# Turning the rounded values by VectorE blocks and DMAs over DRAM instead of the DMA transpose, with the linear layer four places later

## The chip, the core and the metric

The kernel runs on one core of a Trainium2 chip. The core has five engines that run side by side and wait for one another through semaphores: TensorE (PE: matmuls; its weight loads are shown as PEld), VectorE (DVE), ScalarE (ACT), GpSimd (POOL) and SyncE (SP), which issues all the DMAs of this kernel from one queue. The metric is the device time in microseconds (us) of one execution; a comparison takes the median of several runs of each kernel.

## The reference

Sixteen sequences of 256 rows and 256 channels pass through one block: normalise, attention with a mask that leaves 4 sink positions and a window of 32, a projection, and then a linear layer that works on values rounded to 8 bits.

```python
def attention(x, wq, wk, wv, wo):              # x: (16, 256, 256), already normalised
    q = heads(x @ wq.T, 16); k = heads(x @ wk.T, 4); v = heads(x @ wv.T, 4)   # heads of 128
    scores = q @ k.T / sqrt(128)
    mask = (k_pos <= q_pos) & ((k_pos < 4) | (k_pos >= q_pos - 31))
    return merge(masked_softmax(scores, mask) @ v) @ wo.T

def linear(x, weight, bias):                   # x already normalised
    w_scale = max(abs(weight), axis=1) / 127;  w_q = clip(round(weight / w_scale), -128, 127)
    x_scale = maximum(max(abs(x), axis=2) / 127, 1e-12);  x_q = clip(round(x / x_scale), -128, 127)
    return (x_q @ w_q.T) * x_scale * w_scale + bias

x = x + attention(layernorm(x), wq, wk, wv, wo)
x = x + linear(layernorm(x), weight, bias)
```

## The kernel before

The work is cut into 128 units: 16 sequences (n), 4 groups of heads (g), 2 tiles of 128 rows (t). The main loop at the end of the kernel (line 915) walks over them; its index i is called a place here, and a sequence takes 8 places (`PER`). What belongs to other sequences is hung into the places by `at(slot, f, what)`: `small` steps run at the end of a place, `begin` steps early in it, after the read of the weights that the place before wrote, and `close` steps only in the last place. Behind place 124 the `small` steps run in the middle of the place, before the weights are normalised. Every engine runs its instructions in the order in which they were written down (`in_written_order`).

In a place, PE computes the scores of its unit (`pss`, line 560), parts of the output projection of earlier units (`py`), the attention outputs of the unit two places back (`po`, line 623), in every second place a chunk of keys or values (`pk`, `pv`) of the coming sequence, and two heads of its queries (`pq`). Most products are done with seven block products in place of eight, whose sums VectorE and POOL put together (lines 306 to 310). VectorE takes the scores out (571), finds their maximum (573), ScalarE takes the exponentials (598), VectorE divides (605 to 617) and turns the weights in blocks of 32x32 (582). The turned weights travel through DRAM: `zd<-z` (584) at the end of the place, `ad<-zd` (588) early in the next; `po` uses `ad` another place later. The units from 123 on are turned by PE instead (`ptd`, line 565, interleaved with the scores) and used in the very next place.

The normalised input of a coming sequence (`xn`) is turned the same way by `turned_by_blocks`: a block transpose on VectorE (389), four DMAs out to DRAM (394), and, one place later, four DMAs back (403). The first two sequences are turned on PE.

The linear layer of a finished sequence n is `ffn_steps(n)`: statistics, norm (193), scale (714), rounding (721 on VectorE, clamp and subtraction on POOL, 724 and 725, the latter into a bf16 tile `h16`), a transposing DMA from `h16` into `hT` (728), four bf16 matmuls against the rounded weights (`pa`, 739), two evictions on VectorE (`y`, 744), an addition on POOL (745) and the store (746). These six steps stand 4, 5, 6, 8, 9 and 10 places after the end of the sequence. For n = 14 they stand in the places 124 to 127, with the transpose among the `begin` steps of 127 and the matmuls among its `close` steps. The last sequence, 15, has a path of its own (`last_steps`).

Of the kernel before, what the change touches and what calls it, by code (L numbers as in the profile page):

```python
# [9 lines left out]
FP = mybir.dt.float32  # L10
BF = mybir.dt.bfloat16
# [23 lines left out]
def kernel(  # L35
# [12 lines left out]
    pe, dve, act, pool, sp = nc.tensor, nc.vector, nc.scalar, nc.gpsimd, nc.sync  # L48
    B, T, DM = x.shape
    P = 128  # L50
# [4 lines left out]
    NC = DM // P  # L55
    NT = T // P
# [4 lines left out]
    QB = 32  # L61
# [9 lines left out]
    SCALE = 1.0 / math.sqrt(D)  # L71

    const = ctx.enter_context(tc.tile_pool(name="const", bufs=1))
    xp = ctx.enter_context(tc.tile_pool(name="xp", bufs=5))
    p1 = ctx.enter_context(tc.tile_pool(name="p1", bufs=1))
    p2 = ctx.enter_context(tc.tile_pool(name="p2", bufs=2))
    p3 = ctx.enter_context(tc.tile_pool(name="p3", bufs=3))
    dram = ctx.enter_context(tc.tile_pool(name="dram", bufs=3, space=bass.MemoryType.DRAM))
# [4 lines left out]
    ps_m = ctx.enter_context(tc.tile_pool(name="ps_m", bufs=2, space=bass.MemoryType.PSUM))  # L83
# [40 lines left out]
    ident16 = const.tile([P, P], BF, name="ident16")  # L124
# [53 lines left out]
    def statistics(src, tiles, tag, eng=pool):  # L178

        st = p2.tile([P, NT, nc.vector.BN_STATS_DIM], FP, tag="st", name=f"st_{tag}")  # L180
        mv = p3.tile([P, NT, nc.vector.BN_AGGR_DIM], FP, tag="mv", name=f"mv_{tag}")
        for j in tiles:
            dve.bn_stats(st[:, j, :], src[:, j, :])
        for j in tiles:
            dve.bn_aggr(mv[:, j, :], st[:, j, :])
        js = slice(tiles[0], tiles[-1] + 1)
        eng.tensor_scalar(mv[:, js, 1], mv[:, js, 1], LN_EPS, None, ALU.add)
        pool.tensor_tensor(mv[:, js, 1], mv[:, js, 1], half[:, js], ALU.pow)
        return mv

    def standardise(dst, src, mv, tiles):
        for j in tiles:
            dve.tensor_scalar(dst[:, j, :], src[:, j, :], mv[:, j, 0:1], mv[:, j, 1:2], ALU.subtract, ALU.mult)


    wqfT = const.tile([P, NC, DM], BF, name="wqfT")
# [139 lines left out]
    xns, xnT, qt, kt, vw, xn_sums, mvs = {}, {}, {}, {}, {}, {}, {}  # L336
# [22 lines left out]
    def norm_steps(n):  # L359
        def stats():  # L360
            mvs[n] = statistics(xts[n], range(NT), f"a{n}")

        def norm(t):
            if t == 0:
                xns[n] = p1.tile([P, NT, DM], FP, tag="xn", name=f"xn_{n}")
            standardise(xns[n], xts[n], mvs[n], [t])

        return [stats, lambda: norm(0), lambda: norm(1)]

    def channels(n):  # L370

        xn_sums[n] = p2.tile([P, 4, P], FP, tag="xs4", name=f"xs4_{n}")
        b = xn_blocks(n)
        right_sums([xn_sums[n][:, i] for i in range(4)], *b[0], *b[1])

    def turned(n):
        xnT[n] = p2.tile([P, NC, T], FP, tag="xnT", name=f"xnT_{n}")
        pt = ps_m.tile([P, NC, T], FP, tag="m", name=f"xt_{n}")
        for c in range(NC):
            for j in range(NT):  # L380
                pe.transpose(pt[:, c, j * P : (j + 1) * P], xns[n][:, j, c * P : (c + 1) * P], ident)
        dve.tensor_copy(xnT[n], pt)
        channels(n)

    def turned_by_blocks(n):


        z = p1.tile([P, NQ, NT * NC, QB], FP, tag="zx", name=f"zx_{n}")
        dve.transpose(z, xns[n].rearrange("p t (c q i) -> p q (t c) i", c=NC, q=NQ))
        zd = dram.tile([P, NQ, NT * NC, QB], FP, tag="zx", name=f"zxd_{n}")  # L390

        def out():
            for a in range(NQ):
                sp.dma_start(
                    zd[:, a].rearrange("(q j) k i -> j q (k i)", q=NQ),
                    z[a * QB : (a + 1) * QB].rearrange("j q k i -> j q (k i)"),
                )

        def back():
            xnT[n] = p2.tile([P, NC, T], FP, tag="xnT", name=f"xnT_{n}")  # L400
            for t in range(NT):
                for c in range(NC):
                    sp.dma_start(
                        xnT[n][:, c, t * P : (t + 1) * P].rearrange("p (a i) -> p a i", a=NQ), zd[:, :, t * NC + c]
                    )

        return out, back

    NQ = P // QB
# [285 lines left out]
    def ffn_steps(n):  # L695
        xt = xts[n]
        tiles, tag = range(NT), f"{n}"
        h = p1.tile([P, NT, DM], FP, tag="h", name=f"h_{tag}")
        h16 = p1.tile([P, NT, DM], BF, tag="h16", name=f"h16_{tag}")
        xs = p2.tile([P, NT], FP, tag="xs", name=f"xs_{tag}")  # L700
        hT = p1.tile([P, NT, NC, P], BF, tag="hT", name=f"hT_{tag}")
        y = p1.tile([P, NT, DM], FP, tag="yo", name=f"y_{tag}")
        got = []

        def stats():
            got.append(statistics(xt, tiles, f"f{tag}"))

        def norm():
            standardise(h, xt, got[0], tiles)
            if n < B - 2:  # L710
                add_bias(pool)

        def scale():
            dve.tensor_reduce(xs, h, AX.X, ALU.max, apply_absolute_value=True)
            dve.tensor_scalar(xs, xs, 1.0 / 127.0, 1e-12, ALU.mult, ALU.max)

        def quantise():
            xr = p2.tile([P, NT], FP, tag="xr", name=f"xr_{tag}")
            dve.reciprocal(xr, xs)
            for j in tiles:  # L720
                dve.scalar_tensor_tensor(
                    h[:, j, :], h[:, j, :], xr[:, j : j + 1], magic.to_broadcast([P, DM]), ALU.mult, ALU.add
                )
            pool.tensor_scalar(h, h, MAGIC + 127.0, MAGIC - 128.0, ALU.min, ALU.max)
            pool.tensor_scalar(h16, h, MAGIC, None, ALU.subtract)

        def turn():
            sp.dma_start_transpose(
                hT.rearrange("p j c t -> p (j c) t"), h16.rearrange("p j d -> p (j d)")
            )  # L730

        def add_bias(eng):
            eng.tensor_add(xt, xt, bias_bc.unsqueeze(1).to_broadcast([P, NT, DM]))

        def linear():
            pa = ps_m.tile([P, NT, DM], FP, tag="m", name=f"pa_{tag}")
            for j in tiles:
                for c in range(NC):
                    pe.matmul(  # L739
                        pa[:, j, :], hT[:, j, c], wqfT[:, c, :],  # L740
                        start=(c == 0), stop=(c == NC - 1),
                    )
            for j in tiles:
                dve.scalar_tensor_tensor(y[:, j, :], pa[:, j, :], xs[:, j : j + 1], wsc_bc, ALU.mult, ALU.mult)
            pool.tensor_add(y, y, xt)
            sp.dma_start(out_v[n], y)

        return [stats, norm, scale, quantise, turn, linear, lambda: add_bias(dve)]

    def last_steps(j):  # L750

# [72 lines left out]
    begin, close, chunks, early, asked, shares, small, later = {}, {}, {}, {}, {}, {}, {}, {}  # L824

    def at(slot, f, what=small):
        what.setdefault(slot, []).append(f)

    for n in range(B):
        q = (-3, -2, -1, 0, 1, 2, 3, 4)  # L830
        if n == 0:
            q = (-1, -1, 0, 0, 1, 1, 2, 4)
# [10 lines left out]
    for n in range(1, B):  # L843
        first = n * PER - 14
        places = (0, 1, 1, 2) if n == 1 else (4, 5, 6, 7) if n == 2 else (first - 2, first + 2, first + 4, first + 5)
        for k, slot in enumerate(places[:3]):
            at(slot, lambda n=n, k=k: norm_steps(n)[k]())
        if n == 1:
            at(places[3], lambda n=n: turned(n))
        else:  # L850
            def turn(n=n, slot=places[3]):
                for k, f in enumerate(turned_by_blocks(n)):
                    at(slot + 1 + k, f, begin)
                at(slot + 2, lambda: channels(n))

            at(places[3], turn)
            at(max(first - 4, 0), lambda n=n: load_x(n))
# [19 lines left out]
    for n in range(B - 1):  # L877
        done = (n + 1) * PER

        slots = (4, 5, 6, 8, 9, 10) if n < B - 2 else (4, 5, 6, 6, 7, 7, 7)  # L880
        for k, slot in enumerate(slots):
            def step(n=n, k=k):
                if k == 0:
                    steps[n] = ffn_steps(n)
                steps[n][k]()
            at(done + slot, step, begin if k == 4 and n == B - 2 else close if k == 5 and n == B - 2 else small)


    warm = ps_m.tile([P, P], FP, tag="m", name="warm")
# [25 lines left out]
    for i in range(len(units) + 2):  # L915
# [43 lines left out]
        for n, h in asked.pop(i, []):  # L959
            f = queries(n, h)  # L960
# [57 lines left out]
```

## Time and profile before

| | us |
|---|---|
| median of three runs | 769.09 (767.9 to 769.29) |
| the profiled execution | 767.44 |
| its span, first to last instruction | 765.7 |
| PE, share of the chain that ended last | 96% |
| one sequence in the middle | 46.1 |
| in it: PE, VectorE, POOL, ScalarE busy | 46.1, 39.3, 32.2, 24.5 |
| DMA engines busy in the middle | 45% |

A profile line of the timeline gives start, duration, engine, source line, operation, what is written from what, the number of merged instructions, and in brackets the idle time before it and what ended it. A line of the groups gives the shapes, the count, the busy time, the mean duration in ns, and the idle time ahead of the group. A line of the waits gives the total, the number and the longest. A line that lists one tile's instructions gives the shortest, median and longest duration in ns and the first and last start. SP's lines are the issuing of a DMA, not its landing.

### The profile page before, as it was taken

To read this page: it belongs to the slowest core of one execution; us is meant where nothing else is said; L and a number is where in the kernel's file an instruction comes from. 1 tells how busy PE (TensorE), PEld (TensorE's weight loads), DVE (VectorE), ACT (ScalarE), POOL (GpSimd) and SP (SyncE) were. 2 spreads that over 40 slices of the span, in tenths; PEclk is the share of its full clock that TensorE was granted. 3 is DMA by queue.
4 is the path that set the end of the run, shared out by engine and by line. 5 is a ranking of instruction groups with operands and counts; after the bars stand their busy time and mean duration, and the time that the engine had idled before them with its cause. 6 is when DMAs were issued, how large, how long until landed. Compare 5 with 4: busy or idle time off the path is not lost.

```text
span 765.7 us, 18824 instructions
## 1 busy us (share of the span) xinstructions
PE 754.4 (99%) x6483; PEld 742.4 (97%) x6483; DVE 621.8 (81%) x1775; ACT 399.2 (52%) x1561; POOL 511.7 (67%) x812
## 2 busy tenths in 40 slices
PE   9999999999999999999999999999999999999995
PEld 7999999999999999999999999999999999999994
DVE  2588888888888888888888888888888888778765
ACT  3555555555455454555555455554545555455551
POOL 4666977676675867757676675866758676675622
PEclk9999999999999999999999999999999999999998
DMA  7634354344544425445344543436344354443310
GB/s 241 215 102 129 106 147 140 107 124 118 154 124 133 131 90 163 128 137 144 100 125 128 147 141 123 129 96 163 120 145 135 99 136 128 130 137 105 100 40 31
DMA packets 150679, 97.45 MB, mean 127 GB/s; under 512 B 44984, under 2 KB 148792, under 8 KB 150584
## 3 DMA queue, kind: packets, MB, share of 16 engines
q1 hardware_dynamic: 150584, 96.24, 42.8%
q8 instruction: 52, 0.85, 0.5%
q14 instruction: 43, 0.35, 0.2%
HBM read 54.39 MB, written 39.85 MB: 123 GB/s over the span
## 4 chain that ended last, share of the span: by engine, by line
PE 96%; DVE 2%; DMA 1%; ACT 0%; POOL 0%; issue 0%; DVEq 0%; POOLq 0%; ACTq 0%
PE pq L527 24%; PE py L678 23%; PE po L623 15%; PE pss L560 14%; PE pk L495 6%; PE pv L507 6%; PE py L662 3%; PE pq L538 2%; PE pa L739 1%; DMA ad<-zd 1%; PE warm L891 1%; PE pv L470 0%; PE pk L461 0%; PE ptd L565 0%; ACT scores L598 0%
## 5 line engine op out<-in xcount | busy, mean ns | idle before, releaser
L598 ACT ACTIVATE scores<-scores,nmax 128x68 f32<-128x68 f32 x512 | 173.5, 340 | 247.2 <-DVE nmax L573 244.8
L623 PE MATMUL po<-ad,vw 96*128 96x128 f32 x1024 | 135.4, 275 | 0.4 <-DMA ad<-zd 0.4
L560 PE MATMUL pss<-kt,qt 128*128 128x68 f32 x1024 | 130.2, 268 | 0.0
L623 PEld LDWEIGHTS po<-ad,vw 96*128 96x128 f32 x1024 | 125.6, 192 | 1.5 <-DMA ad<-zd 0.5
L560 PEld LDWEIGHTS pss<-kt,qt 128*128 128x128 f32 x1024 | 126.1, 192 | 0.7 <-issue 0.5
L527 PE MATMUL pq<-xs,wq_sums 128*128 128x128 f32 x714 | 118.6, 275 | 0.0
L571 DVE SCALAR_TENSOR_TENSOR scores<-pss,masks 128x272 f32<-128x272 f32 x128 | 56.2, 439 | 63.7 <-PE pss L560 60.8
L527 PEld LDWEIGHTS pq<-xs,wq_sums 128*128 128x128 f32 x714 | 98.8, 192 | 0.0
L598 ACT ACTIVATION_READ_ACCUMULATOR scores<-scores,nmax 128x1 f32 x512 | 95.6, 187 | 0.0
L635 ACT COPY oT<-po 128x512 f32<-128x512 f32 x129 | 75.4, 585 | 23.0 <-PE po L623 23.0
L678 PE MATMUL py<-wo_sums,os 128*128 128x128 f32 x672 | 87.0, 279 | 0.0
L257 POOL TENSOR_TENSOR os<-oT 128x256 f32<-128x256 f32 x56 | 41.0, 732 | 58.0 <-ACT oT L635 58.0
L678 PEld LDWEIGHTS py<-wo_sums,os 128*128 128x128 f32 x672 | 79.5, 192 | 0.0
L306 POOL TENSOR_TENSOR ktmp<-b_k 128x256 f32<-128x256 f32 x30 | 22.4, 746 | 84.3 <-ACT b_k L327 84.3
L527 PE MATMUL pq<-xnT,wq_sb 128*128 128x128 f32 x476 | 72.7, 275 | 0.1
L582 DVE STREAM_TRANSPOSE z<-scores 128x384 f32<-128x384 f32 x120 | 69.4, 578 | 4.1
L617 DVE TENSOR_TENSOR scores<-scores,sm 128x272 f32<-128x272 f32 x120 | 60.3, 503 | 4.1
L527 PEld LDWEIGHTS pq<-xnT,wq_sb 128*128 128x128 f32 x476 | 62.7, 192 | 0.2 <-PE pv L507 0.2
L678 PE MATMUL py<-wo_sb,oT 128*128 128x128 f32 x448 | 62.0, 281 | 0.0
L573 DVE TENSOR_REDUCE nmax<-scores 128x4 f32<-128x272 f32 x128 | 55.8, 436 | 4.4
L678 PEld LDWEIGHTS py<-wo_sb,oT 128*128 128x128 f32 x448 | 54.5, 192 | 0.0
L308 DVE TENSOR_TENSOR qt<-pq,qt 128x256 f32<-128x256 f32 x119 | 50.5, 424 | 4.0
(187 smaller groups left out, 1700.4 us busy)
## 6 DMA issues: line engine op xcount, KB each, us to landing
zd<-z SPq DMA_DIRECT2D x120, 192.0 KB
ad<-zd SPq DMA_DIRECT2D x120, 192.0 KB
vd<-vt SPq DMA_DIRECT2D x30, 256.0 KB
vw<-vd SPq DMA_DIRECT2D x30, 256.0 KB
vw<-vd SPq DMA_DIRECT2D x30, 224.0 KB
x<-in_x_dram SPq DMA_DIRECT2D x15, 256.0 KB
out_dram<-y SPq DMA_DIRECT2D x15, 256.0 KB
zxd<-zx SPq DMA_DIRECT2D x56, 64.0 KB
```

The source lines that it names most:

```text
L308: eng.tensor_add(c21_c22, like(p[1][:, 0:2], c21_c22), v.unsqueeze(1).to_broadcast(c21_c22.shape))
L495: pe.matmul(to, left, right, start=True, stop=True)
L527: pe.matmul(to, left, right, start=True, stop=True)
L560: pe.matmul(pss[:, k, :], qt[n, g][:, t, k].rearrange("p h i -> p (h i)"), kt[n, g][:, t * NBLK + k, :], start=True, stop=True,)
L571: dve.scalar_tensor_tensor(s[:, :, 0:NK], pss, SCALE, masks[:, t], ALU.mult, ALU.add)
L573: dve.tensor_reduce(nmax, s[:, :, 0:NK], AX.X, ALU.max, negate=True)
L582: dve.transpose(z, s.rearrange("p k (c i) -> p c k i", c=NCH))
L598: act.activation(s[:, k, 0:NK], s[:, k, 0:NK], AF.Exp, bias=nmax[:, k : k + 1], scale=1.0, accum_out=sm[:, k : k + 1],)
L617: dve.tensor_mul(s, s, sm.unsqueeze(2).to_broadcast([P, NBLK, NK]))
L623: pe.matmul(po[:, k], vw[n, g // 2][:, t * NBLK + k, g % 2 * D : (g % 2 + 1) * D], ad[:, :, k], start=True, stop=True,)
L635: act.copy(o[:, t, hs].rearrange("p h (k i) -> p k h i", i=QB), po[:, :, hs])
L678: pe.matmul(region(py, i), left[:, e], right[:, e], start=(g == 0 and e == 0 and i in (1, 4)), stop=(g == G - 1 and e == 1 and i in (7, 3)),)
```

## The change

The rounded values of the sequences 0 to 13 are no longer narrowed to bf16 by POOL and transposed by a DMA. POOL leaves them in f32 in place. VectorE turns them in blocks of 32x32 (the same helper as for the normalised input, now with the source, the pool and a tag as arguments), four DMAs carry them out to DRAM and four back, and ScalarE narrows the result to bf16 (`narrow`). That takes nine steps instead of six; they stand 4, 5, 6, 8, 10, 11, 12, 13 and 14 places after the end of the sequence, so that the matmuls stand at 14 in place of 10. For n = 13 the turn and all after it stand one place earlier, and the matmuls at place 125 (112 + 13). Sequence 14 keeps the bf16 tile and is turned by four PE transposes at the beginning of place 127, narrowed by ScalarE out of PSUM. The pool of inputs `x` gets a sixth buffer, since an input is held longer. The layout of `hT` changes from row tile first to channel half first.

```diff
-    xp = ctx.enter_context(tc.tile_pool(name="xp", bufs=5))
+    xp = ctx.enter_context(tc.tile_pool(name="xp", bufs=6))
...
-    def turned_by_blocks(n):
+    def turned_by_blocks(src, pool_of, tag):
-        z = p1.tile([P, NQ, NT * NC, QB], FP, tag="zx", name=f"zx_{n}")
-        dve.transpose(z, xns[n].rearrange("p t (c q i) -> p q (t c) i", c=NC, q=NQ))
-        zd = dram.tile([P, NQ, NT * NC, QB], FP, tag="zx", name=f"zxd_{n}")
+        z = p1.tile([P, NQ, NT * NC, QB], FP, tag="zx", name=f"z_{tag}")
+        dve.transpose(z, src.rearrange("p t (c q i) -> p q (t c) i", c=NC, q=NQ))
+        zd = dram.tile([P, NQ, NT * NC, QB], FP, tag="zx", name=f"zd_{tag}")
...
         def back():
-            xnT[n] = p2.tile([P, NC, T], FP, tag="xnT", name=f"xnT_{n}")
+            to = pool_of.tile([P, NC, T], FP, tag=tag.split("_")[0], name=tag)
             for t in range(NT):
                 for c in range(NC):
                     sp.dma_start(
-                        xnT[n][:, c, t * P : (t + 1) * P].rearrange("p (a i) -> p a i", a=NQ), zd[:, :, t * NC + c]
+                        to[:, c, t * P : (t + 1) * P].rearrange("p (a i) -> p a i", a=NQ), zd[:, :, t * NC + c]
                     )
+            return to
...
-        h16 = p1.tile([P, NT, DM], BF, tag="h16", name=f"h16_{tag}")
+        h16 = p1.tile([P, NT, DM], BF, tag="h16", name=f"h16_{tag}") if n == B - 2 else h
-        hT = p1.tile([P, NT, NC, P], BF, tag="hT", name=f"hT_{tag}")
+        hT = p1.tile([P, NC, T], BF, tag="hT", name=f"hT_{tag}")
...
+        way = []
+
         def turn():
-            sp.dma_start_transpose(
-                hT.rearrange("p j c t -> p (j c) t"), h16.rearrange("p j d -> p (j d)")
-            )
+            if n < B - 2:
+                way.extend(turned_by_blocks(h, p1, f"hb_{tag}"))
+                return
+            pt = ps_m.tile([P, NC, T], BF, tag="m", name=f"ht_{tag}")
+            for c in range(NC):
+                for j in tiles:
+                    pe.transpose(pt[:, c, j * P : (j + 1) * P], h16[:, j, c * P : (c + 1) * P], ident16)
+            way.append(pt)
+
+        def out():
+            way[0]()
+
+        def back():
+            way.append(way[1]())
+
+        def narrow():
+            act.copy(hT, way[-1])
...
-                        pa[:, j, :], hT[:, j, c], wqfT[:, c, :],
+                        pa[:, j, :], hT[:, c, j * P : (j + 1) * P], wqfT[:, c, :],
...
-        return [stats, norm, scale, quantise, turn, linear, lambda: add_bias(dve)]
+        if n < B - 2:
+            return [stats, norm, scale, quantise, turn, out, back, narrow, linear]
+        return [stats, norm, scale, quantise, turn, narrow, linear, lambda: add_bias(dve)]
...
-        slots = (4, 5, 6, 8, 9, 10) if n < B - 2 else (4, 5, 6, 6, 7, 7, 7)
+        slots = (4, 5, 6, 8, 10, 11, 12, 13, 14) if n < B - 2 else (4, 5, 6, 6, 7, 7, 7, 7)
+        if n == B - 3:
+            slots = (4, 5, 6, 8, 9, 10, 11, 12, 13)
         for k, slot in enumerate(slots):
...
-            at(done + slot, step, begin if k == 4 and n == B - 2 else close if k == 5 and n == B - 2 else small)
+            if n < B - 2:
+                at(done + slot, step, begin if k in (5, 6) else small)
+            else:
+                at(done + slot, step, begin if k == 4 else close if k == 6 else small)
```

More of the change, by code (lines that the diff above doesn't have):

```diff
@@ L851, in turn @@
             def turn(n=n, slot=places[3]):
-                for k, f in enumerate(turned_by_blocks(n)):
-                    at(slot + 1 + k, f, begin)
+                out, back = turned_by_blocks(xns[n], p2, f"xnT_{n}")
+                at(slot + 1, out, begin)
+                at(slot + 2, lambda: xnT.__setitem__(n, back()), begin)
                 at(slot + 2, lambda: channels(n))
```

## The prediction

> **What bounds the kernel now.** I read the engines' totals first, then what TensorE (PE) waited for, then the stretch in which each edit lands, then the last 40 us. The totals, with the list of PE's waits:
>
> ```profile
> PE 754.4 (99%) x6483; PEld 742.4 (97%) x6483; DVE 621.8 (81%) x1775; ACT 399.2 (52%) x1561; POOL 511.7 (67%) x812
> ...
> PE ht_last L791 <- DVE d_last L784: 4.3, 3, 2.9
> PE warm L891 <- POOL half L132: 1.3, 1, 1.3
> PE po L623 <- DMA ad<-zd: 0.4, 1, 0.4
> PE pv L507 <- DVE qt L307: 0.3, 1, 0.3
> ```
>
> The sequences in the middle all take 46.1 us, and PE is busy for all of it: in the table of stretches of 46.10 us from 192.20 to 607.10, every one has 46.10 us of PE. The four waits make 6.3 us, and 5.6 of these lie at the start and the end. So in the middle there is nothing to win except one wait of 0.36 us; whatever an edit makes PE wait is paid in full. The pieces that the change takes away or copies:
>
> ```profile
> L728 SPq DMA_TRANSPOSE hT<-h x15: 1223/1249/1558, 116.5 to 744.8; - x15
> L725 POOL TENSOR_SCALAR h<-h 128x512 bf16<-128x512 f32 x15 | 22.7, 1516 | 1.2
> L389 DVE STREAM_TRANSPOSE zx<-xn 128x512 f32<-128x512 f32 x14 | 9.4, 669 | 0.0
> 430.12 1.93 SPq L394 DMA_DIRECT2D zxd<-zx  x4
> 435.36 3.50 SPq L403 DMA_DIRECT2D xnT<-zxd  x4
> L227 PE MATMUL wt<-ident,wq x4: 219/219/219, 80.6 to 80.7; 128*128 128x128 bf16 x4
> ```
>
> The reader is to see that every new operation of sequences 0 to 13 already exists for xn, with its price, and that none of them is on PE.
>
> **The middle, edit by edit.** I call the loop's index a place; eight places are one sequence, and r is the place modulo 8.
>
> VectorE gains one block transpose, 14 x 0.67 = 9.4 us, at r = 2. There it was idle for 1.59 us before y (L744) and that y is now gone from r = 2: hidden. Without that cover it would delay the eviction of the scores (L571) by 0.67 us. For sequence 13 it stands at r = 1, where the idle time was 0.46 us: 0.2 us late on VectorE, with 1.59 us to catch up in the next place.
>
> POOL: the subtraction writes f32 in place; I price it as the f32 clamp beside it (L724, 0.614) instead of 1.516. A gain of 0.9 us that POOL does not need.
>
> ScalarE gains 14 narrowing copies of 128x512, 0.59 us each by the row of L635, at r = 5 behind the four key copies. There it was idle for 1.39 us before the exponentials of the next place: hidden, with 0.8 us to spare. Its input, the four returns, is issued some 6 us earlier, and the like returns at 389.43 had the DMA engines busy until about 393.5, 4 us later.
>
> SyncE's queue: the transpose (1.25 us at r = 1) goes; four stores (1.93) come at r = 3 and four returns (2.61 to 3.50) at r = 4, each behind the read of ad and ahead of the next zd, the three vw reads and the next ad. At r = 0 and 1 the same eight stand before the same zd and ad, and the po that uses those ads came 6 us after their issue with no wait. At r = 3 and 4 it comes 6.7 and 6.2 us after. Hidden; bounds 0 to 0.3 us per sequence, value 0.
>
> The linear layer: 4 matmuls, 0.44 us of PE, leave r = 2 and enter r = 6. PE loses nothing. Both places hold a values chunk, so the same banks are in rotation, and VectorE has 0.99 + 0.44 us of room for y (0.88) before the scores of r = 7. But the store of out moves too, past the load of x, and it stands ahead of the read of ad that is already the tightest:
>
> ```profile
> 402.45 0.39 SPq L746 DMA_DIRECT2D out_dram<-y  x1
> 402.96 0.39 SPq L588 DMA_DIRECT2D ad<-zd  x1
> ...
> 424.54 0.37 SPq L512 DMA_DIRECT2D vd<-vt  x1
> 424.96 0.46 SPq L94 DMA_DIRECT2D x<-in_x_dram  x1
> 425.52 0.43 SPq L588 DMA_DIRECT2D ad<-zd  x1
> ...
> 176.14 1.16 PE L623 MATMUL po<-ad,vw 96*128 96x128 f32 x8 [0.36 <-DMA ad<-zd]
> ```
>
> Issue to use is 3.7 us with out before it (402.96 to 406.66) and 4.04 with x before it (425.52 to 429.56). In the new r = 7 both stand before it. POOL's y follows the values' sums, 424.5 + 1.27 = 425.8, so ad is issued at about 426.3 and used at 429.56 + 0.43 = 430.0: 3.7 us again, with 256 KB more in front. At the 340 GB/s that the windows show for such a burst these take 0.8 us. The burst of vd, x and ad began 425.25; with out in it ad is through by about 428.6, 1.4 us early, where the old r = 3 had 1.9. One of 14 old reads overran that (the 0.36 us). I take back the 0.36 us and put one or two new overruns of the like in, +0.3; the bounds are 0 and one in each of the ten places with both x and out, 10 x 0.36 = 3.6.
>
> [...]
>
> **The tail, where the cost is.** Two edits land in the last sequence's places, where each place waits for the weights of the place before.
>
> (a) Sequence 14 is turned on PE: 4 bf16 transposes at place 127. The four of L227 took 0.40 us together in the trace. PE has no gap there (744.84 is the next matmul), and the rounded values end on POOL at 744.80, so it also can't come earlier. +0.4; bounds 0.4 and 4 x 0.22 = 0.9.
>
> (b) Sequence 13's linear layer moves from place 122 to place 125, and from place 125 on the small steps run in the middle of a place, before the weights are normalised. There VectorE meets y (L744) ahead of the norm of sequence 14 and ahead of the weights' own chain:
>
> ```profile
> 735.23 0.72 DVE L193 TENSOR_SCALAR h<-x,mv_f 128x256 f32<-128x256 f32 x2
> 736.89 0.16 DVE L605 TENSOR_TENSOR sm<-sm,floor 128x4 f32<-128x4 f32 x1 [0.93 <-ACT scores L598]
> 737.30 0.69 DVE L611 TENSOR_TENSOR z<-scores,sm 128x384 f32<-128x384 f32 x1
> ...
> 735.61 1.89 PE L662 MATMUL py<-wo_sb,oT 128*128 128x256 f32 x8
> 737.34 1.06 PE L623 MATMUL po<-ad,vw 96*128 96x128 f32 x8
> 738.40 0.27 PE L565 MATMUL ptd<-ident,z 128*96 128x128 f32 x1
> ```
>
> Working: PE reaches this point 0.43 us sooner, since place 122 lost its 4 matmuls. The projection of 8 then ends, and pa starts, at 737.34 - 0.43 = 736.91. y started 0.64 us after pa in each pair that I looked at (398.86 to 399.50, 749.19 to 749.83): 737.55. Behind y are queued: y itself 0.88, to 738.43; the norm 0.72, to 739.15; then L605 to the end of L611, 1.10, to 740.25. PE, with po after pa, is at the transpose of z (L565) at 738.40 as before, and z is 1.9 us late. The four score matmuls of the place are interleaved with these transposes, so the next scores are late as well, and with them the next exponentials and z: nothing downstream has 1.9 us of slack (z of place 126 ended 743.52, its transpose came 743.88). +1.9; the upper bound takes the 0.43 not regained, 2.3; the lower, if y lay wholly in the idle 0.93 us, is 0.
>
> **Sum.** -0.36 + 0.3 + 0.4 + 1.9 = +2.2 us, on a span of 765.7: 767.9, and 769.6 for the profiled execution (767.44). The median of the runs, 769.09, lies 1.65 above that execution, so 769.09 + 2.2 = 771.3. What a measurement of this kernel can tell from no change is 0.2%, 1.5 us: "same" is 767.6 to 770.6.
>
> **Rivals.**
> 1. Late weights in the middle as well: x, values and out in one burst before the tight ad at r = 7. For it: the slack shrinks from 1.9 to 1.4 us and one read already overran. Against: 13 of 14 did not. With ten overruns, 771.3 + 3.3 = 774.6.
> 2. The tail absorbs the move: y finds the idle 0.93 us and PE loses only its transposes and an overrun or two: 0 + 0.4 + 0.3 - 0.4, 769.4. For it: PE arrives 0.43 us early. Against: y needs pa, and pa stands behind fourteen matmuls of the projection.
> 3. Faster: the runs' median is 1.65 us above the profiled execution. If these are overruns at r = 3, behind the store of out, then the change takes them away, because there ad no longer waits for POOL's y (it is issued 1.3 us sooner), and so much falls off the path in the middle. That decides if the tail costs less than 1.6: 769.09 - 1.65 - 0.36 + 0.4 = 767.5. Against: the profile shows a single 0.36 us wait, and the tail stall stands in written order.
> 4. The transposing DMA was slowing the others, so that it does more than it says: nothing in the middle waits, so this is worth 0 there; it falls together with 2.
>
> **How the numbers follow.** My forecast (b) with small overruns, 770.0 to 773.3: 0.56. Rival 1: 0.17. Rivals 2 and 4: 0.19. Rival 3: 0.08. The range runs from just under rival 2 to rival 1, 768.8 to 774.6. Faster than 767.6 is rival 3, 0.08; within 0.2% is rivals 2 and 4 with the low end of the forecast, 0.19 + 0.05 = 0.24; slower is the rest, 0.68.
>
> **What would show it.** In the profile after: a wait of PE at ptd (L565) near 739 for z, some 1.9 us; DVE idle before y for pa of about 2 us in the same place; the last four transposes 0.4 us of PE; middle sequences still 46.1 us; PE's waits for ad at r = 0 (the use of the read issued at r = 7) in none to three sequences. I am wrong if y at place 125 runs before 736, if middle sequences lengthen by 0.3 us or more, or if ScalarE waits for the returns.

## The result and the profile after

| | before | after |
|---|---|---|
| median of the runs, us | 768.55 (767.90 to 769.29) | 776.00 (774.75 to 781.38) |
| the profiled execution | 767.44 | 774.75 |
| its span | 765.7 | 773.0 |

The change makes the kernel slower: 1.0108 times the time before, 95% interval 1.0088 to 1.0129. The forecast was slower, 771.3 in a range of 768.8 to 774.6; the measured 7.5 us are more than three times the 2.2 that the sum gave, and 776.00 lies outside the range. (The forecast stood on a median before of 769.09, of three runs; a fourth makes it 768.55.) The runs after the change also lie further apart, 6.6 us instead of 1.4.

Line numbers in the views after the change are those of the changed kernel: L566, L612 and L624 are the lines 565, 611 and 623 of the kernel above, L756 and L761 its lines 739 and 744. The first view is what TensorE waited for in the changed kernel (total us, times, longest):

```profile
PE ht_last L810 <- DVE d_last L803: 4.4, 3, 2.9
PE ptd L566 <- DVE z L612: 2.6, 1, 2.6
PE po L624 <- DMA ad<-zd: 1.9, 2, 1.7
PE warm L916 <- POOL half L132: 1.3, 1, 1.3
```

The first and last lines were there before. Two are new or grown: a wait for the weights z in the tail, 2.6 us, and waits for the read-back weights `ad`, 1.9 us instead of 0.4. The second view is the timeline around the tail's wait, TensorE first, then VectorE:

```profile
740.01 0.60 PE L756 MATMUL pa<-wqfT,hT 128*128 128x256 bf16 x4
740.45 1.06 PE L624 MATMUL po<-ad,vw 96*128 96x128 f32 x8
744.25 0.28 PE L566 MATMUL ptd<-ident,z 128*96 128x128 f32 x1 [2.58 <-DVE z L612]
745.31 5.21 PE L663 MATMUL py<-wo_sb,oT 128*128 128x256 f32 x16
...
740.65 0.88 DVE L761 SCALAR_TENSOR_TENSOR y<-pa,xs,wsc_bc 128x256 f32<-128x256 f32 x2 [2.66 <-PE pa L756]
741.44 1.68 DVE L193 TENSOR_SCALAR h<-x,mv_f 128x256 f32<-128x256 f32 x2
743.44 0.67 DVE L612 TENSOR_TENSOR z<-scores,sm 128x384 f32<-128x384 f32 x1
```

Read it downwards on VectorE: y of sequence 13 stands idle for 2.66 us until its matmuls come, the norm of sequence 14 queues behind it, z behind the norm, and TensorE's transpose of z stands idle for 2.58 us. Then the line that I had not expected: the 16 projection matmuls take 5.21 us, where the same 16 took 3.62 in the kernel before:

```profile
739.36 3.62 PE L662 MATMUL py<-wo_sb,oT 128*128 128x256 f32 x16
```

The table of stretches tells why (length; busy us with number of instructions on PE, PEld, DVE, ACT and POOL; the granted TensorE clock; DMA share and GB/s):

```profile
741.60:744.20 2.60, 0.08 (x1) 0.00 (x0) 2.44 (x5) 0.58 (x1) 1.37 (x1) 1.00 0.11 37
745.30:748.70 3.40, 3.40 (x11) 2.71 (x10) 3.15 (x10) 2.03 (x9) 0.45 (x1) 0.53 0.00 0
```

After 2.6 us with nothing to do, TensorE gets a granted clock of 0.53 for 3.4 us. That is another 1.6 us for these 16. Scores of place 126 began 3.1 us later than before (738.23, 741.34), those of place 127 already 7.5 us later (743.71, 751.25): of the whole loss, 4.4 us arise in this one place.

The rest arises in the middle. The starts of the places, compared with those of the kernel before, show how: late reads of `ad` put 2.4 us into the places 40 and 88, each place 7 of 13 sequences is about 0.10 us longer, 1.35 in all, and the wait that the kernel before had at place 28 is gone, 0.5 less. This is the queue and TensorE around the longest wait for `ad`:

```profile
516.95 0.38 SPq L513 DMA_DIRECT2D vd<-vt  x1
517.38 0.46 SPq L94 DMA_DIRECT2D x<-in_x_dram  x1
518.18 0.38 SPq L763 DMA_DIRECT2D out_dram<-y  x1
518.65 0.42 SPq L589 DMA_DIRECT2D ad<-zd  x1
...
524.35 1.16 PE L624 MATMUL po<-ad,vw 96*128 96x128 f32 x8 [1.67 <-DMA ad<-zd]
```

The order is the one that the prediction worked out: values, x, out, then the read of `ad`. TensorE would have used it at 524.35 - 1.67 = 522.7, 4.0 us after its issue, and it was not there.

The new operations themselves cost what the rows before said, or were hidden as costed:

```profile
L389 DVE STREAM_TRANSPOSE z_hb<-h x14: 668/670/671, 120.5 to 718.5; 128x512 f32<-128x512 f32 x14
L747 ACT CAST hT<-hb x14: 615/616/622, 138.5 to 736.5; 128x512 bf16<-128x512 f32 x14
L726 POOL TENSOR_SCALAR h<-h 128x512 f32<-128x512 f32 x14 | 21.0, 1499 | 1.2
752.38 0.39 PE L737 MATMUL ht<-ident,h 128*128 128x128 bf16 x4
752.60 1.95 PE L663 MATMUL py<-wo_sb,oT 128*128 128x256 f32 x8
```

The block transpose takes 0.67 us, the narrowing 0.62. The subtraction on POOL is not cheaper with an f32 result: 1.50 us. The four transposes of sequence 14 hold TensorE for 0.22 us, from 752.38 to the next matmul at 752.60.

### The profile page after: what moved, and what is told of

Same layout as the page of the kernel before. It is cut to its first block, busy times and chain, and to the rows that moved or that the text cites. A ratio compares the mean times of both kernels' runs of the same rounds, so it can differ in the third digit from the quotient of the medians.

```text
span 773.0 us, 19058 instructions
## 1 busy us (share of the span) xinstructions
PE 757.5 (98%) x6487; PEld 744.6 (96%) x6487; DVE 625.4 (81%) x1789; ACT 404.9 (52%) x1576; POOL 513.2 (66%) x812
## 4 chain that ended last, share of the span: by engine, by line
PE 93%; DMA 3%; DVE 2%; POOL 0%; SPq 0%; issue 0%; ACT 0%; DVEq 0%; POOLq 0%; ACTq 0%
PE pq L528 24%; PE py L679 23%; PE po L624 14%; PE pss L561 13%; PE pk L496 6%; PE pv L508 6%; PE py L663 3%; PE pq L539 1%; DMA ad<-zd 1%; PE pa L756 1%; DMA vp<-vt 1%; DMA wo_sb<-in_woT_dram 1%; PE pv L471 0%; DMA x<-in_x_dram 0%; PE ptd L566 0%
## 5 line engine op out<-in xcount | busy, mean ns | idle before, releaser
L624 PE MATMUL po<-ad,vw 96*128 96x128 f32 x1024 | 135.4, 275 | 1.9 <-DMA ad<-zd 1.9
L624 PEld LDWEIGHTS po<-ad,vw 96*128 96x128 f32 x1024 | 125.6, 192 | 3.0 <-DMA ad<-zd 2.3
L257 POOL TENSOR_TENSOR os<-oT 128x256 f32<-128x256 f32 x56 | 43.3, 774 | 63.2 <-ACT oT L636 63.2
```

Of the source, the lines that this page charges most:

```text
L624: pe.matmul(po[:, k], vw[n, g // 2][:, t * NBLK + k, g % 2 * D : (g % 2 + 1) * D], ad[:, :, k], start=True, stop=True,)
```

## The experiments

My theory after this view: three costs that add up, (1) the tail's wait with the low clock behind it, (2) late reads of `ad` behind the burst, (3) the small delay in place 7 of each sequence. The rivals: the blocks and their DMAs cost the time; the clock falls for a reason of its own. All medians below stand beside runs of the kernel before whose medians lay between 767.7 and 768.4.

| run | what differs from the changed kernel | median, us | ratio to before, 95% |
|---|---|---|---|
| e0 | nothing | 775.62 | 1.0107 (1.0091 to 1.0123) |
| e1 | sequence 13's linear layer last in its place | 771.26 | 1.0040 (1.0028 to 1.0052) |
| e2 | x one place earlier | 773.04 | 1.0069 (1.0057 to 1.0081) |
| e3 | DMA transpose again, places kept | 776.32 | 1.0113 (1.0093 to 1.0132) |
| e4 | 22 idle-time matmuls at place 126 | 777.93 | 1.0123 (1.0109 to 1.0138) |
| e8 | 11 of them | 773.92 | 1.0080 (1.0067 to 1.0093) |
| e5 | all linear layers last in their places | 773.07 | 1.0058 (1.0045 to 1.0070) |
| e6 | e5 and e2 | 768.80 | 1.0011 (1.0002 to 1.0021) |
| e10 | e1 and e2 | 769.03 | 1.0006 (0.9997 to 1.0015) |
| e11 | e6 once more, beside e10 | 768.76 | 1.0010 (0.9999 to 1.0020) |
| e7 | four DRAM buffers for the weights | 777.19 | 1.0114 (1.0093 to 1.0135) |
| e9 | four DRAM buffers for the values | 775.64 | 1.0121 (1.0094 to 1.0147) |

**The changed kernel again (e0).**

> The changed kernel as it is, five rounds. Theory: its extra time is the wait at place 126 for the weights of place 125 (2.6 us), the halved TensorE clock that follows it (1.6 us) and a varying number of late reads of ad, so the runs of this kernel spread by 2 to 6 us where those of the kernel before spread by 1.4, and the profile shows the 2.6 us wait and the clock at 0.5 again, at the same place. Rival: the profiled 2.6 us wait and the low clock were chance; then they are absent or elsewhere in this profile.

The runs spread from 773.48 to 778.29. The profiled one has the same idle gap at place 126, but not the low clock after it:

```profile
PE ptd L566 <- DVE z L612: 2.6, 1, 2.6
PE po L624 <- DMA ad<-zd: 1.5, 3, 0.8
...
741.80:744.40 2.60, 0.05 (x1) 0.01 (x1) 2.41 (x5) 0.56 (x1) 1.34 (x1) 1.00 0.12 41
745.50:748.90 3.40, 3.40 (x18) 2.99 (x17) 3.19 (x10) 2.03 (x9) 0.50 (x1) 1.00 0.00 0
```

In the same 3.4 us after the gap 18 matmuls ran here and 11 in the execution shown above. So the wait comes every time, and the low clock in part of the runs: the expected low clock in this profile did not come.

**Sequence 13's linear layer last in its place (e1).**

```diff
-                at(done + slot, step, begin if k in (5, 6) else small)
+                at(done + slot, step, begin if k in (5, 6) else later if n == B - 3 and k == 8 else small)
```

> Only the linear layer of sequence 13 is moved within place 125, from ahead of the norm and the weights to the end of the place. Theory (the wait at place 126 and the clock after it are one cost): both vanish, 4.2 us less than the changed kernel, about 771.8. Rival A (the clock drops for a reason of its own): 2.6 us less, 773.4. Rival B (the tail has slack and the middle costs it all): less than 1 us.

775.62 - 771.26 = 4.4 us less, where 4.2 were expected and 2.6 without the clock. TensorE no longer waits for z. VectorE in the same place:

```profile
739.06 0.73 DVE L193 TENSOR_SCALAR h<-x,mv_f 128x256 f32<-128x256 f32 x2
741.13 0.68 DVE L612 TENSOR_TENSOR z<-scores,sm 128x384 f32<-128x384 f32 x1
742.70 0.88 DVE L761 SCALAR_TENSOR_TENSOR y<-pa,xs,wsc_bc 128x256 f32<-128x256 f32 x2 [0.89 <-PE pa L756]
```

The norm and z go first, y fills idle time behind them, and the stretch after it runs at full clock. The norm takes 0.73 us here and 1.68 in the changed kernel, where POOL's addition of y ran at the same time:

```profile
741.60 1.37 POOL L762 TENSOR_TENSOR y<-y,x 128x512 f32<-128x512 f32 x1 [4.95 <-DVE y L761]
```

Of the two instructions of the norm, the first, begun before the addition, took 0.40 us as in e1, and the second, begun just after it, 1.36. So 0.95 us more on VectorE stand beside 1.37 us of POOL. The trace of the kernel before shows the like: the norm took 0.72 us at 735.23, with POOL idle, and 1.21 us at 415.71, its first instruction 0.40 beside POOL's L257 and its second, from 416.04, 0.88 beside L258, begun at 416.05. Why the second takes longer there, no run here shows.

**x one place earlier (e2).**

```diff
-            at(max(first - 4, 0), lambda n=n: load_x(n))
+            at(max(first - 5, 0), lambda n=n: load_x(n))
```

> Only the load of x is issued one place earlier, so that it no longer stands in one burst with the values, the store of out and the tight read of ad. Theory (the burst makes ad late): no wait of TensorE for ad in the middle, 1.9 us less than the profiled 774.75, and the runs spread less, 1.5 us or under. Rival (ad is late because it is issued behind the store of out, not for the bytes of x): one or two waits for ad remain and the time moves by less than 0.5 us.

2.6 us less. The list of TensorE's waits no longer has `ad` (two delays ahead of `po`, of 0.3 and 0.4 us, remain at the places 40 and 120). The queue at the same place:

```profile
517.20 0.37 SPq L513 DMA_DIRECT2D vd<-vt  x1
518.43 0.39 SPq L763 DMA_DIRECT2D out_dram<-y  x1
518.91 0.42 SPq L589 DMA_DIRECT2D ad<-zd  x1
```

`ad` is issued as late as in the changed kernel, 1.6 us ahead of the place's first scores in both, and still behind the store of out, so the rival, which blamed the issue, falls. What is gone from in front of it is x. The spread did not shrink to 1.5 us (771.96 to 775.37): the tail's wait and its low clock are still in this kernel, and the mean clock of its runs goes from 0.992 to 0.997.

**The turning alone undone (e3).**

```diff
-                way.extend(turned_by_blocks(h, p1, f"hb_{tag}"))
+                sp.dma_start_transpose(hx.rearrange("p j c t -> p (j c) t"), h16.rearrange("p j d -> p (j d)"))
...
```

The lines left out bring back the two bf16 tiles and leave the steps `out`, `back` and `narrow` of these sequences empty.

> The turning alone is undone: the sequences 0 to 13 have the DMA transpose and the bf16 tile again, but the linear layer stays at its new places, sequence 14 is turned on TensorE and x keeps its sixth buffer. Theory (the places cost the time, not the blocks and their eight DMAs): same as the changed kernel within 1 us, the 2.6 us wait and the low clock still there. Rival (the blocks, their DMAs in the queue and VectorE's 9.4 us cost it): 3 us or more faster than the changed kernel.

776.32, the same as the changed kernel, with the same waits:

```profile
PE po L624 <- DMA ad<-zd: 2.9, 3, 1.4
PE ptd L566 <- DVE z L612: 2.6, 1, 2.6
```

Neither the blocks on VectorE nor the eight DMAs in the queue cost time that can be seen; the places do. This is the run that rules the main rival out.

**Matmuls in the idle time (e4, e8).** One scores matmul is repeated at place 126, between the first scores and the first transpose of z; its result is the same.

```diff
+            if w and units.index(w) == len(units) - 3 and k == 0:
+                for _ in range(22):
+                    pe.matmul(
+                        pss[:, k, :], qt[n, g][:, t, k].rearrange("p h i -> p (h i)"),
+                        kt[n, g][:, t * NBLK + k, :], start=True, stop=True,
+                    )
```

> The changed kernel with 22 more repetitions of one scores matmul at place 126, 2.3 us of TensorE work with the same result, in the 2.6 us in which it waited for z. Theory (the idle time brings the clock down some microseconds later, in part of the runs): the wait stays, short or gone as idle time, the clock is 1.00 from 744 to 749 in the profile, and every run has a mean clock of 0.996 or more unless another wait does the same; the slowest runs (778 to 781) go, the median falls by about 1, to 774.6. Rival (the clock falls by itself at this point of the program): clock 0.5 again in some runs and the same spread.

This one was mis-sized. Each of these matmuls shows as two records, and the 22 took 4.9 us (44 records), more than the wait, so the median rose by 2.3 us. It says only that the clock did not fall behind place 126 here; that every run would have a mean clock of 0.996 or more did not come (the profiled one has 0.994, from a fall near the end of the kernel). So it was done with 11:

> As the run with the repeated scores matmul, with 11 repetitions: there 22 took 4.9 us of TensorE, two passes each, 2.3 us more than the wait, and the median rose by 2.3. 11 take 2.45 us, inside the 2.6 us wait. Theory (the clock falls because TensorE stood idle): TensorE is done with them before z comes, so the tail costs as much as in the changed kernel without its low clock: 1.00 from 744 to 749 in the profile, a median of 774.5 to 775.5, no run above 777. Rival (the clock falls on its own there): clock 0.5 after place 126 in some run, a median of 775.6 or more and runs to 778.

```profile
743.94 2.62 PE L567 MATMUL pss<-kt,qt 128*128 128x68 f32 x22
746.69 0.29 PE L572 MATMUL ptd<-ident,z 128*96 128x128 f32 x1
...
743.90:746.60 2.70, 2.66 (x25) 2.52 (x23) 2.58 (x6) 0.58 (x1) 1.37 (x1) 1.00 0.09 31
747.60:751.00 3.40, 3.40 (x19) 3.01 (x18) 3.04 (x10) 2.03 (x9) 0.33 (x1) 1.00 0.00 0
```

The transpose still comes only when z is there, and the clock stays at 1.00. The profiles price the two parts. From the first scores of place 126 to those of place 127 it takes 5.48 us in the kernel before and in e1, and 8.24 here. Six kernels have the idle gap (the changed one, e0, e2, e3, e7, e9). In the profiles of e0, e3 and e9, where the clock stayed at 1.00, it takes 8.22 or 8.23; in those of the changed kernel, e2 and e7, where the clock was 0.53 to 0.58 for 3.4 us behind the gap, 9.91. So the wait costs 2.75 us and the low clock, where it comes, 1.7 more. In none of the eight profiles without the gap did the clock fall there.

Among the runs, a mean clock of 0.992 or lower, 775 to 781 us, came in 7 of the 28 of the kernels with the gap and in no other kernel; 0.994 and 0.995 came without it too, in 10 of 28 runs of e5, e6 and e11. In all six runs of e8 it was 0.996 or 0.997. Its median fell to 773.92, 1.7 us under e0 (expected was 774.5 to 775.5; the two intervals just touch), and no run passed 775.83. So the idle gap can make the clock fall, and filling it with work that nobody needs kept the clock up and was, at the edge of what the intervals separate, faster than leaving it idle.

**Every linear layer last in its place (e5), and with x earlier (e6).** The linear layers go into a list that runs behind the other small steps; e6 adds the edit of e2.

```diff
-                at(done + slot, step, begin if k in (5, 6) else small)
+                at(done + slot, step, begin if k in (5, 6) else behind if k == 8 else small)
...
         small_steps(i)
+        for f in behind.pop(i, []):
+            f()
```

> Every linear layer of the sequences 0 to 13 goes to the end of its place, behind all other small steps. Theory: as the run that moved only sequence 13's (771.26), and the 0.1 us that each place 7 of a sequence lost goes too, because VectorE takes the maximum for the rounding of the next sequence before it waits for the matmuls; 13 x 0.1 = 1.3 us less, 770.0. Waits for ad stay (2 to 5 of them). Rival (the 0.1 us belongs to the extra y on VectorE wherever it stands): 771.3, and a sequence still costs 0.1 us more than before.

773.07 instead of the expected 770.0: the third cost did not come out in the time. The 0.1 us steps at place 7 are gone from the profile, but the waits for `ad` are the longest of all profiles, 3.3 us in three, and three of its five runs had a mean clock of 0.994.

> Both: each linear layer last in its place, and x loaded one place earlier. Theory (three separate costs: tail, place 7, late ad): 2.0 us less than with the linear layer alone, 768 to 768.5, even with the kernel before (767.86) within 0.2%, and a spread of 1.4 or less. Rival (something of the blocks and their DMAs is still unpaid): 770 or more.

768.80, 1.0011 times the kernel before, with an interval to 1.0021: 0.3 us above what was expected, and about what a measurement can tell from no change. The spread did not shrink as expected (767.41 to 771.38); four of the twelve runs had a mean clock of 0.994 or 0.995, in the profiled one because the clock was 0.50 from 756.0 to 759.3, behind a wait of 1.27 us for the last sequence's rounding. e10 has the same wait (1.28 us) and a clock of 1.00 behind it.

**The third cost alone (e10, e11).** e10 has the edits of e1 and e2, so that the layers of the sequences 0 to 12 stay ahead of the next sequence's maximum; e11 is e6 again, beside it.

> Sequence 13's linear layer last in its place and x one place earlier; the linear layers of the others stay ahead of the next sequence's maximum. It differs from the run with both edits (768.8) only in that. Theory (VectorE's wait for the matmuls at place 6 costs 0.1 us a sequence in the time too): 13 x 0.1 = 1.3 us more, about 770.1, and steps of 0.1 at each place 7 in the profile. Rival (that 0.1 is taken up elsewhere): 768.8.

> The kernel with every linear layer last in its place and x one place earlier once more, on the same chip and beside the same runs of the kernel before, so that the difference of the two is read within one set. Theory: 1.3 us less than the run that keeps the other layers ahead, and within 0.2% of the kernel before. Rival: the two differ by less than 0.5 us.

769.03 and 768.76: the rival holds, the 1.3 us do not show. Place by place, e10 does lose 0.10 to 0.12 us against the kernel before in each place 7, 1.4 us over the run, but its list of waits has none for `ad`, and that of e11, without those steps, has two (0.9 us):

```profile
PE ht_last L810 <- DVE d_last L803: 4.4, 3, 2.9
PE po L624 <- DMA ad<-zd: 0.9, 2, 0.5
```

The four profiles with x earlier agree: with the steps (e2, e10) late reads delay the places by 0.7 and 0.4 us in all, without them (e6, e11) by 1.7 each. So the delay seems to give the late read the time that it lacks, and taken away, most of it comes back as that wait; four single executions fit this and do not prove it. No version was measurably faster than the kernel before, and e10, nearest to it at 1.0006 (0.9997 to 1.0015), keeps every part of the change.

**Which reads are late (e7, e9).** In the profiles of the late layer almost all waits stand at the places 40, 64 and 88, every 24th (one at 16, and outside the period one at 108 in e3 and one at 120 in e11). Three DRAM buffers against eight places give that period.

```diff
-        zd = dram.tile([P, NCH * P], FP, tag="zd", name=f"zd_{n}_{g}_{t}")
+        zd = dram4.tile([P, NCH * P], FP, tag="zd", name=f"zd_{n}_{g}_{t}")
...
```

The line left out opens `dram4`, a DRAM pool with four buffers.

> The changed kernel with four DRAM buffers for the weights instead of three. In all profiles of the late layer the waits for ad stand at the places 40, 64 and 88 or next to them, every 24th: three buffers against eight places a sequence. Theory (which of the three DRAM buffers is read beside the burst decides if ad is late): with four buffers every sequence meets the same buffer, so the waits come in every sequence or in none. Rival (the period is that of another buffer with three turns, the values' or the blocks'): waits at 40, 64 and 88 as before.

> The changed kernel with four DRAM buffers for the values instead of three. Theory (the period of 24 places in the late reads of ad is the values' buffers, two a sequence over three): the waits leave the places 40, 64 and 88 or come every second sequence. Rival (it is the blocks' buffers or the addresses of x and out): waits at 40, 64 and 88 as before.

e7 does this for the weights, e9 the same for the values. With four buffers for the weights the waits stay at 64 and 88, with four for the values at 40, 64 and 88. Neither buffer makes the period. What does stays open: the blocks' DRAM buffers, the addresses of x and out, or `ad` itself, whose tiles in SBUF also take turns among three buffers (pool `p3`), which no run varied.

## Why the prediction was wrong

- The middle's bound was read rightly: TensorE has no slack there, and every wait was paid. The hidden parts were hidden (e3): the block transposes, the eight DMAs, the narrowing. Pricing POOL's subtraction at 0.614 us was wrong, 1.50 measured, at no cost.
- The place and the direction were right: z of place 125 was late behind y and the norm, and the shown VectorE order is the one of the working. The step that failed is the size of (b), +1.9, on two counts. It priced the norm from a row where POOL was idle (0.72; with POOL's addition beside it, 1.68), so the wait was 2.6 and cost 2.75. And it took the wait for the whole cost: the low clock behind it, 1.7 us more where it comes, was not in the sum, though the clock row of the page before already had an 8 in its last slice. Undoing this step gives 4.4 us.
- The second term that failed is the +0.3 for late reads behind x, out and values. The mechanism was rival 1's; its price of 0.36 us an overrun came from the single one in the trace before, and its chance from 1 in 14. The nine profiles of kernels with the late layer and x at its old place have one to four, up to 1.95 us. Undoing it gives 2.6 us. The -0.36 for the old overrun was right in kind: the wait at place 28 is gone.
- The two undone together (e10) leave 0.6 us over the kernel before, within what a measurement can tell. The parts 4.4 and 2.6 make 7.0 of the 7.8 us between e0 and its runs of before.
- "VectorE has 0.99 + 0.44 us of room for y" was wrong in its order: y stands in the queue ahead of the next sequence's maximum (0.67), which used to fill that room. It shows as 0.1 us a sequence in the profile, 1.4 us in all, a cost that the sum put at nothing. Undoing it (e11 against e10) moved the median by only 0.3 us, as late reads came back.
- The +0.4 for sequence 14's transposes was 0.22.
- Rivals 2 and 3 fell with the wait at place 126; rival 4 with e3, where the transposing DMA is back and nothing gets slower or faster. ScalarE waited for no return in the place of the narrowing: L747 stands in none of its waits.

## What to carry to other kernels

A step moved to a later place moves into another queue order: list what is written down behind it on its engine, above all an instruction that waits for a late matmul, and put such a step last in its place. A wait on a TensorE that was never idle can cost more than its length: here a gap of 2.6 us was followed, in three of six profiles, by 3.4 us at about half the clock, 1.7 us more. A read that is just in time should have no other load in the burst before it, even if it is issued no earlier: moving x out of it took 2.6 us off here (e2).

## What was not expected of the hardware

- An idle gap of 2.6 us was followed by 3.4 us at a granted clock of 0.53 in one execution and by a clock of 1.00 in another of the same kernel; with 11 matmuls of no use in the gap the mean clock stayed at 0.996 or more in six runs of six, and the median was 1.7 us shorter. In e6 a gap of 1.27 us was followed by 3.3 us at 0.50.
- The late reads keep a period of 24 places that neither the weights' nor the values' DRAM buffers explain.
- POOL's subtraction of one constant from 128x512 values takes 1.50 us, with a bf16 or an f32 result, and the two-sided clamp of the same values 0.61.
